# Preparing the next layer's first block inside the last image of the layer before it

## The chip, the cores and the metric

One core of one Trainium2 chip runs the whole program. The metric is the time of one execution on the device in microseconds (us), as the median of several runs. The engines are TensorE (PE), VectorE (DVE), ScalarE (ACT), GpSimd (POOL) and SyncE (SP), which here only issues DMA transfers. Each engine runs its own instructions strictly in order.

## The reference

The input x has shape (4, 56, 56, 128), and all is in float32. Four layers follow one another; the change lies at the seam between the first two.

```python
x = x + _L0_conv_ref(_gn(x), ...)     # layer 0: neighbourhood attention, 4 heads, 7x7 windows
x = x + _L1_conv_ref(_gn(x), ...)     # layer 1: two Mamba blocks, one after the other
t = _to_tokens(x)
t = t + _L2_attn_ref(_ln_t(t), ...)   # layer 2: additive (tanh) attention, then a mixture
t = t + _L2_ffn_ref(_ln_t(t), ...)
t = t + _L3_attn_ref(_ln_t(t))        # layer 3: attention, then a mixture of 8 experts
t = t + _L3_ffn_ref(_ln_t(t), ...)
```

`_gn` is a group norm over 32 groups of 4 channels. Each image has statistics of its own, so layer 1 can begin on image 0 as soon as layer 0 has finished image 0. One Mamba block of layer 1, cut to what matters:

```python
xz = h @ in_w;  u, res = split(xz, 2)
u = silu(causal_conv4(u) + cb)              # 4 taps along a row
dt, Bm, Cm = split(u @ xw, [8, 24])
delta = softplus(dt @ dtw + dtb)
h_t = exp(delta * A) * h_(t-1) + (delta * u) * Bm     # the scan, 256 channels x 16 states
y = sum over states (h_t * Cm) + u * D
return (y * silu(res)) @ ow
```

## The kernel before, in words

An image is held as 28 tiles of 112 rows and is worked on in chunks of 4 tiles (448 tokens, 8 image rows), so there are 7 chunks per image and 28 in all. The engines' instructions are placed by hand: the program's order is each engine's order, except that a few first instructions of layer 1 which depend on nothing late slip into the end of layer 0.

**Layer 0.** Each chunk k is split into two units, by columns; 56 units in all. The loop over positions i does, in this order: the scores of unit i+1 on PE (`scores`); steps listed in `early` and `turns`; their exponentials on ACT and their product with a bias table, 3 heads on DVE and 1 on POOL (`weights`); steps listed in `mid`; the weighted sums of unit i-1 on PE (`sums`); steps listed in `at`. The lists are filled ahead of the loop with queries, keys and values of later chunks; with `finish` of earlier ones, which copies the sums on ACT, divides on DVE, projects on PE and adds to X on DVE; with the group norm of the next image (`norm_steps`); and with the building of layer 1's weights on DVE (`next_weights`, 42 steps spread over 50 positions from position 4 on). The last image occupies units 42 to 55. During it, `next_norm` takes the statistics of image 0 for layer 1: 7 turns (4 transposes on PE and one statistics instruction on DVE each) at positions 42 to 48, and the group sums and the square root after them. Queries, keys, values, turns and projections share two PSUM buffers named m, in order of issue. The normalized images `xnT` lie in two buffers of the pool `l0_big`; the three bias tables tab0 to tab2 lie in `l0_w`.

**Layer 1.** A block is one chunk of one image in one of the two Mamba layers: 56 blocks, in groups of 4 and 3 chunks. Each block has 16 pairs, a pair being two sets of 8 channels with 16 states each on 128 partitions. The loop over pairs p does: the fetch of pair p+4 by DMA (E from delta_dram, or V from du_dram for 3 pairs in 16); the spreading of du on PE and the exponential of E on ACT for pair p+2 (`select`); the product with Bm on DVE for pair p+1 (`inputs`); the scan on DVE and the product with Cm on POOL for pair p (`scan`). `mamba_pre` prepares a block while the 16 pairs of the block before it run: convolution (`conv`, `conved`), SiLU, x projection (`xproj`, `dbl`), four spreads on PE with their copies (`spread`, `parts`, `spreaded`), softplus (`delta`), the product du on POOL, eight stores of du and delta to DRAM on SP (`du`), and the gate branch (`res`, `resed`). Its steps are dealt to positions relative to the block; for block 0 there are no pairs beside which they could run, so the loop begins at pair -19 and the first scan comes at pair 0.

The buffers of a block (us, delta, du, bc, sres) are in the pool `l1_sm`, two of each, used in turn; raw, raw_res and dbl have one each.

Of the kernel before, what the change touches and what calls it, by code (L numbers as in the profile page):

```python
# [20 lines left out]
P = 128  # L21
# [13 lines left out]
BW = 8  # L35
# [103 lines left out]
class Hybrid:  # L139
# [59 lines left out]
    def group_norm(self, b, pool, group):  # L199
# [12 lines left out]
        def place_bands(pool):  # L212

            g.xn = self.t(pool, [P, BANDS, HW, BW], "xnT")
            g.chunk = lambda c: g.xn[:, :, c * SEQ : (c + 1) * SEQ, :].rearrange(
                "p b s j -> p b (s j)"
            )
# [83 lines left out]
    def bias_tables(self, pool, tmp, room, m, groups):  # L301

        nc, a = self.nc, self.a
        N = sum(WIDTHS)
        K = BW * (1 + KR)
        rpb = self.load(tmp, [NH * KR, KR], "rpb", a["L0_conv_rpb"].rearrange("h r d -> (h r) d"))
        same = self.load(tmp, [K, BW], "same", a["k_same"])
        cols = self.load(tmp, [K, N], "cols", a["k_cols"])  # L310
        kill = self.load(tmp, [TP, 3 * SEQ], "kill", a["k_kill"])
        tables = [self.t(pool, [TP, NH, SEQ, N], f"tab{k}") for k in range(3)]
        often = self.t(tmp, [NH * KR, BW, 1 + KR], "rpb_often")
        nc.vector.memset(often, 1.0)
        span = ROWS + SEQ - 1 + 2 * NB
        r = {}

        def spread():

            r["rows"] = by_row = room()[:K, : NH * span * BW].rearrange(  # L320
                "p (h r k) -> p h r k", h=NH, k=BW
            )
            nc.gpsimd.memset(by_row, 0.0)
            nc.vector.tensor_copy(
                often[:, :, 0:KR], rpb.unsqueeze(1).to_broadcast([NH * KR, BW, KR])
            )
            ps = m()
            nc.tensor.transpose(
                ps[:K, : NH * KR], often.rearrange("p k d -> p (k d)"),
                self.ident[: NH * KR, : NH * KR],  # L330
            )
            for h in range(NH):
                nc.vector.tensor_tensor(
                    by_row[:, h, SEQ - 1 : SEQ - 1 + KR, :],
                    ps[:K, h * KR : (h + 1) * KR].unsqueeze(2).to_broadcast([K, KR, BW]),
                    same.unsqueeze(1).to_broadcast([K, KR, BW]), op=ALU.mult,
                )

        def table(kind, i):

            ps = groups()[:, : NH * N].rearrange("p (h n) -> p h n", h=NH)
            at = SEQ - 1 - i + (2 - kind) * NB
            for h in range(NH):
                nc.tensor.matmul(
                    ps[:, h, :], r["rows"][:, h, at : at + ROWS, :].rearrange("p r k -> p (r k)"), cols,
                    start=True, stop=True,
                )
            nc.scalar.activation(
                tables[kind][:, :, i, :], ps, AF.Exp, bias=kill[:, kind * SEQ + i : kind * SEQ + i + 1]
            )  # L350

        return tables, spread, table

    def layer0(self, wp1):
# [5 lines left out]
        with ExitStack() as ctx:  # L360
            wp = ctx.enter_context(tc.tile_pool(name="l0_w", bufs=1))
            big = ctx.enter_context(tc.tile_pool(name="l0_big", bufs=2))
# [39 lines left out]
            def norm_steps(b):  # L402
                g = self.group_norm(b, big, group)

                def chunk(c):
                    if c == 0:
                        g.place_bands(big)
                    g.turn(c, m)
                    g.stats(c)
                    return lambda: g.raw_bands(c)  # L410
# [14 lines left out]
            def next_norm():  # L425
                g = self.first_norm = self.group_norm(0, wp1, group)
                parts = g.groups(m)
                both = lambda fs: lambda: [f() for f in fs]
                def chunk(c):
                    return lambda: (g.turn(c, m), g.stats(c)) and None  # L430

                return (
                    [chunk(c) for c in range(NCH)]
                    + [parts[0], both(parts[1:3]), both(parts[3:5]), parts[5]]
                )
# [155 lines left out]
            for k, (b, c) in enumerate(chunks):  # L591
                if c == 0:
                    for n, step in enumerate(norm_steps(b + 1) if b + 1 < B else next_norm()):
                        add(first[k] + n, step, to=turns if n < NCH else at)
# [11 lines left out]
            for n, step in enumerate(next_weights):  # L606
                add(first[2] + n * 50 // len(next_weights), step)
# [124 lines left out]
    def layer1(self):  # L732
# [5 lines left out]
        with ExitStack() as ctx:  # L738
# [4 lines left out]
            dr = ctx.enter_context(tc.tile_pool(name="l1_dram", bufs=2, space=DRAM))  # L743
# [14 lines left out]
            h = {}  # L758
            pre, yg, E, D, V, HS, py = {}, {}, {}, {}, {}, {}, {}
# [147 lines left out]
            for j, block in enumerate(order):  # L907
# [24 lines left out]
                head, tail = self.mamba_pre(pre, j, block, h, w, sm, m, dr)  # L932
                for steps, to in ((head, first), (tail, last)):
                    for i, step in steps:
                        add(to, at - PAIRS + i, step)
            g = self.first_norm
            g.place(big, DC - 1)
            hand_over(0, g)
            for c in range(NCH):
                turned = lambda c=c: (g.turn(c, m), g.scaled(c, g.ps))  # L940
                if c == 0:
                    turned()
                else:
                    add(last, (-PAIRS + 9, 2, 10, 12, PAIRS + 2, PAIRS + 10)[c - 1], turned)
            for n, step in enumerate(self.first_stats()):
                add(first if n < 20 else last, n_pairs if n < 20 else n_pairs + 10, step)
            for p in range(-PAIRS - 3, n_pairs + PAIRS):
# [18 lines left out]
    def mamba_pre(self, pre, j, block, h, w, sm, m, dr):  # L966


        nc = self.nc
        b, c, l = block  # L970
        seqs = lambda ap: ap.rearrange("p (s t) -> p s t", t=HW)
        r = pre[j] = {}
        ps = {}

# [8 lines left out]
        def conved(f):  # L983
            if f == 0:
                r["raw"] = self.t(sm, [P, NHALF, CH], "raw", bufs=1)
            nc.scalar.activation(r["raw"][:, f], ps[0], AF.Identity, bias=w["cb"][:, l, f : f + 1])

        def silu(of, to):
            r[to] = self.t(sm, [P, NHALF, CH], to)
# [10 lines left out]
        def dbl():  # L1000
            r["dbl"] = self.t(sm, [P, CH], "dbl", bufs=1)
# [7 lines left out]
        def parts(i):  # L1009
            if i == 0:  # L1010
                r["delta"] = self.t(sm, [P, NHALF, CH], "delta")
# [3 lines left out]
        def spreaded(i):  # L1015
            if i == 0:
                r["bc"] = self.t(sm, [P, 2, CH], "bc")
# [5 lines left out]
        def du():  # L1023
            r["du"] = self.t(sm, [P, NHALF, CH], "du")
# [19 lines left out]
        def resed(f):  # L1044
            if f == 0:
                r["raw_res"] = self.t(sm, [P, NHALF, CH], "raw_res", bufs=1)
            nc.scalar.copy(r["raw_res"][:, f], ps[0])

        head = [
            (-1, conved, 0), (1, conved, 1), (2, resed, 0), (4, dbl), (5, parts, 0), (6, parts, 1),  # L1050
            (7, spreaded, 0), (9, spreaded, 1), (12, resed, 1),
        ]
        tail = [(k // 2 - 3, conv, k // DC, k % DC) for k in range(2 * DC)]
        tail += [
            (1, silu, "raw", "us"), (1, res, 0), (3, xproj), (4, spread, 0), (5, spread, 1),
            (6, spread, 2), (7, delta), (7, spread, 3), (8, du), (11, res, 1),
            (PAIRS + 1, silu, "raw_res", "sres"),
        ]
        bind = lambda f, *args: lambda: f(*args)
        return [[(x[0], bind(*x[1:])) for x in xs] for xs in (head, tail)]  # L1060
# [1060 lines left out]
def tile_hybrid(ctx, tc, a, out):  # L2121
    k = Hybrid(ctx, tc, a, out)
    with ExitStack() as ctx1:
        wp = ctx1.enter_context(tc.tile_pool(name="l1_w", bufs=1, reuse_waits="tile"))
        k.layer0(wp)
# [37 lines left out]
```

## Time and profile before

| quantity | value |
|---|---|
| median of 3 runs | 7037.23 us (7028.32 to 7045.93) |
| the profiled execution | 7044.67 us, span 7042.9 us |
| mean granted PE clock | 0.931 |
| PE, DVE, ACT, POOL busy in the span | 86%, 82%, 69%, 41% |
| last addition to X in layer 0 (DVE) begins | 374.23 us |
| first scan of layer 1 (DVE) begins | 409.64 us |
| last pair sums of layer 1 (PE) begin | 2988.7 us |

The granted clock is the share of its full clock at which PE was allowed to run in a stretch. Busy shares over the whole span say little here, since the layers have different limits: in layer 1 DVE is busy almost without a break, in layer 0 it is PE. Positions on the time line count from the start of the span.

### The profile page before, as it was taken

What the parts mean: (1) busy time and instruction counts of PE and PEld (TensorE: products, weight loads), DVE (VectorE), ACT (ScalarE), POOL (GpSimd) and SP (SyncE); (2) the same over time, 40 slices, a digit from 0 to 9 for tenths busy, and PEclk for the clock granted to TensorE, in tenths of its full rate; (3) what the DMA queues carried; (4) which work ended last, traced back from release to release, by engine and by line L of the source; (5) the groups of instructions that cost most, each with busy time, mean ns of one, the idle gap of its engine ahead of it and who ended that gap; (6) DMA issues with size and microseconds to landing.
All of it is one profiled execution on the core that took longest, in us unless ns stands there. A gap on an engine that the chain in (4) does not pass through costs nothing.

```text
span 7042.9 us, 101461 instructions
## 1 busy us (share of the span) xinstructions
PE 6058.3 (86%) x37386; PEld 2624.0 (37%) x37386; DVE 5762.5 (82%) x10108; ACT 4833.4 (69%) x4827; POOL 2853.0 (41%) x1920
## 2 busy tenths in 40 slices
PE   8889999998999999877777777777788899999998
PEld 7733332333232333232233323332333355555554
DVE  6869999999999999977878888888888753566665
ACT  5557767766767677679998998999899833322231
POOL 3359989998999999911010101000101100000000
PEclk9989989998999899889999999999899999999999
DMA  2057767776776777600000000000003304243433
GB/s 53 5 126 188 186 158 188 186 183 169 187 185 174 178 187 186 159 11 3 1 5 4 8 2 5 5 6 3 6 18 116 91 18 145 72 112 92 118 85 94
DMA packets 363446, 654.19 MB, mean 93 GB/s; under 512 B 95412, under 2 KB 211908, under 8 KB 362437
## 3 DMA queue, kind: packets, MB, share of 16 engines
q1 hardware_dynamic: 362949, 647.71, 36.5%
q8 instruction: 295, 4.83, 0.3%
q14 instruction: 202, 1.65, 0.1%
HBM read 536.78 MB, written 104.37 MB: 91 GB/s over the span
## 4 chain that ended last, share of the span: by engine, by line
PE 22%; ACT 12%; DVE 11%; issue 8%; POOL 1%; SPq 0%; DMA 0%; DVEq 0%; ACTq 0%; POOLq 0%
ACT th L1265 10%; PE o L1903 6%; DVE th L1256 6%; PE q L1891 5%; PE s L1279 4%; DVE X L2103 2%; PE pe L2098 2%; ACT e L1293 1%; POOL e L1300 1%; PE o L1309 1%; PE m L1437 1%; DVE wide L1923 1%; PE m L1212 1%; DVE X L1445 0%; PE m L1720 0%
## 5 line engine op out<-in xcount | busy, mean ns | idle before, releaser
L1265 ACT ACTIVATE th<-th 128x5488 f32<-128x5488 f32 (+13 forms) x560 | 2184.6, 3945 | 177.3 <-DVE th L1256 151.0
L1256 DVE TENSOR_SCALAR th<-fT,g 128x784 f32<-128x784 f32 (+13 forms) x3920 | 1868.8, 549 | 306.1 <-PE s L1279 287.7
L846 POOL TENSOR_TENSOR hs<-hs,bc 128x896 f32<-128x896 f32 x896 | 1855.2, 2090 | 125.4 <-DVE hs L841 121.6
L1279 PE MATMUL s<-th,place 128*32 128x392 f32 (+5 forms) x14112 | 1389.4, 488 | 444.5 <-ACT th L1265 441.7
L841 DVE TENSOR_TENSOR_SCAN hs<-E,u 128x896 f32<-128x896 f32 x728 | 1449.6, 2007 | 1.8 <-ACT E L825 1.8
L825 ACT ACTIVATE E<-E,rate 128x448 f32<-128x448 f32 x1456 | 886.0, 661 | 124.1 <-DMA E<-delta_dram 117.0
L1279 PEld LDWEIGHTS s<-th,place 128*32 128x32 f32 (+1 forms) x14112 | 454.1, 111 | 1313.7 <-ACT th L1265 670.4
L787 PE MATMUL u<-du,pick 32*128 32x448 f32 x2912 | 815.9, 628 | 142.7 <-DVE hs L841 139.5
L834 DVE TENSOR_TENSOR u<-u,bc 128x896 f32<-128x896 f32 x728 | 784.0, 1077 | 71.5 <-PE u L787 71.2
L1896 ACT ACTIVATE e<-q,shift 128x448 f32<-128x448 f32 (+1 forms) x511 | 322.5, 634 | 673.5 <-PE q L1891 651.3
L1300 POOL TENSOR_TENSOR e<-e,later 112x112 f32<-112x112 f32 x112 | 154.1, 1376 | 1133.4 <-ACT e L1293 676.3
L2103 DVE SCALAR_TENSOR_TENSOR X<-pe,r_gate,X 112x128 f32<-112x128 f32 x896 | 311.9, 348 | 313.9 <-PE pe L2098 277.9
L852 PE MATMUL y<-hs,sum 128*32 128x448 f32 x3584 | 499.5, 631 | 4.0 <-POOL hs L846 4.0
L1891 PE MATMUL q<-xT 128*128 128x448 f32 (+1 forms) x1022 | 500.8, 572 | 0.9 <-ACT e L1896 0.9
L1903 PE MATMUL o<-e,xk 128*128 128x448 f32 (+1 forms) x1022 | 479.5, 553 | 16.7 <-ACT oT L1868 16.7
L1309 PE MATMUL o<-e,xk 112*128 112x392 f32 (+5 forms) x1024 | 390.0, 501 | 91.2 <-POOL e L1300 87.6
L787 PEld LDWEIGHTS u<-du,pick 32*128 32x128 f32 x2912 | 246.1, 195 | 575.5 <-DVE hs L841 222.3
L1196 POOL MEMSET xa<- 112x4 f32 (+1 forms) x32 | 55.1, 1723 | 972.8 <-PE m L1189 972.8
L2032 POOL MEMSET lc_xa<- 112x4 f32 x28 | 3.1, 110 | 949.1 <-DVE lc_xa L2026 700.2
L834 POOL TENSOR_TENSOR V<-V,bc 128x896 f32<-128x896 f32 x168 | 350.3, 2085 | 12.7 <-DMA V<-du_dram 12.7
L829 ACT ACTIVATE u<-u 128x896 f32<-128x896 f32 x168 | 151.9, 904 | 294.9 <-PE u L778 215.4
L841 DVE TENSOR_TENSOR_SCAN hs<-u,V 128x896 f32<-128x896 f32 x168 | 338.3, 2014 | 0.0
(274 smaller groups left out, 7841.7 us busy)
## 6 DMA issues: line engine op xcount, KB each, us to landing
E<-delta_dram SPq DMA_DIRECT2D x728, 448.0 KB
V<-du_dram SPq DMA_DIRECT2D x168, 448.0 KB
wide<-in_L_ffn_weight SPq DMA_DIRECT2D x64, 1024.0 KB
r<-M SPq DMA_DIRECT2D x189, 224.0 KB
M<-wide SPq DMA_DIRECT2D x72, 392.0 KB
du_dram<-du SPq DMA_DIRECT2D x224, 112.0 KB
delta_dram<-delta SPq DMA_DIRECT2D x224, 112.0 KB
M<-wide SPq DMA_DIRECT2D x72, 168.0 KB
```

Source lines behind the costliest of these rows:

```text
L787: nc.tensor.matmul(halves(to)[:, k], w["pick"][own, q, :], pre[j]["du"][own, f], start=True, stop=True,)
L825: nc.scalar.activation(e, e, AF.Exp, scale=rate)
L834: eng.tensor_mul(v, v, pre[p // PAIRS]["bc"][:, 0:1].to_broadcast([P, 2, CH]))
L841: nc.vector.tensor_tensor_scan(flat, E.pop(p), V.pop(p), 0.0, op0=ALU.mult, op1=ALU.add)
L846: nc.gpsimd.tensor_mul(HS[p], HS[p], bc[:, 1:2].to_broadcast([P, 2, CH]))
L852: nc.tensor.matmul(py[j, f][r * HD : (r + 1) * HD, :], w["sum"][:, q, :], HS[p + r // 2][:, r % 2], start=False, stop=(q == QG - 1),)
L1256: nc.vector.tensor_scalar(th[i][:, s, lo:hi], fT[j][:, lo:hi], g[b, J // WT][:, at : at + 1], None, op0=ALU.add,)
L1265: nc.scalar.activation(own, own, AF.Tanh)
L1279: nc.tensor.matmul(ps[j, J][QW * blk : QW * blk + rows, h, lo:hi], place[:, off : off + rows], z[:, at + s, h * HALF + lo : h * HALF + hi] ...
L1309: nc.tensor.matmul(po[j][:, h, lo:hi], xk[b, J // WT][:, J % WT, :], e[:, h * HALF + lo : h * HALF + hi], start=(J == 0), stop=(J == t + ( ...
L1891: nc.tensor.matmul(ps[:n, :CH], of_tile(xT[b], t), xT[b][:, c * CH : (c + 1) * CH], start=True, stop=True,)
L1903: nc.tensor.matmul(po[b, c], xk[b][:n, t, :], e[:n], start=first, stop=last)
```

## The change

Two tiles of 128 partitions x 3136 elements, room0 and room1, are made in the pool that holds layer 1's weights, so that they live through both layers. In layer 0, room0 holds the normalized images 0 and 2 (`l0_big` has one buffer left, for images 1 and 3), and room1 holds bias table 0. During the last image, `hold_block` takes both rooms over for layer 1. From then on room0 holds us, delta and du of every even block and dbl of all blocks; room1 holds bc and sres of every even block and raw_res of all blocks. Odd blocks have one buffer of each in `l1_sm`. The buffer raw is gone: `conved` writes us, and the SiLU works in place.

`next_norm` is extended by block 0's preparation. Its turns stand at positions 42 to 45, the group norm's steps at 46 to 49, `place` (which normalizes chunk 0 into the part of room0 that will hold du) at 50, then one step per position: conv(0), conv(1), res(0) with the SiLU, res(1), xproj, spread(0), spread(1), spread(2) with softplus, and at 59 du with spread(3). Layer 1's loop begins at pair -4. Layer 1's weights are built over 40 positions instead of 50.

```diff
-            g.xn = self.t(pool, [P, BANDS, HW, BW], "xnT")
+            g.xn = room().rearrange("p (b s j) -> p b s j", b=BANDS, j=BW)
...
-        tables = [self.t(pool, [TP, NH, SEQ, N], f"tab{k}") for k in range(3)]
+        first = self.rooms[1]()[:TP, : NH * SEQ * N].rearrange("p (h s n) -> p h s n", h=NH, s=SEQ)
+        tables = [first] + [self.t(pool, [TP, NH, SEQ, N], f"tab{k}") for k in range(1, 3)]
...
-            big = ctx.enter_context(tc.tile_pool(name="l0_big", bufs=2))
+            big = ctx.enter_context(tc.tile_pool(name="l0_big", bufs=1))
...
-                        g.place_bands(big)
+                        g.place_bands(self.rooms[0] if b % 2 == 0 else lambda: self.t(big, [P, HW * HW], "xnT"))
...
+                def place():
+                    self.hold_block()
+                    rows = self.du_room[:, : SEQ * (DC - 1 + HW)].rearrange(
+                        "p (s t) -> p s t", t=DC - 1 + HW
+                    )
+                    nc.gpsimd.memset(rows[:, :, : DC - 1], 0.0)
+                    g.chunk = lambda c: rows[:, :, DC - 1 :]
+                    g.turn(0, m)
+                    g.scaled(0, g.ps)
+                    self.h[0, 0, 0] = rows
+
+                s = self.first_block = self.mamba_pre(0, (0, 0, 0), None, m)
+                conv = lambda f: lambda: ([s.conv(f, k) for k in range(DC)], s.conved(f))
+                return [
+                    *[chunk(c) for c in range(NCH)],
+                    parts[0], both(parts[1:3]), both(parts[3:5]), parts[5], place,
+                    conv(0), conv(1), lambda: (s.res(0), s.resed(0), s.silu("us")),
+                    lambda: (s.res(1), s.resed(1)), lambda: (s.xproj(), s.dbl()),
+                    lambda: (s.spread(0), s.parts(0)), lambda: (s.spread(1), s.parts(1)),
+                    lambda: (s.spread(2), s.spreaded(0), s.delta()),
+                    lambda: (s.du(), s.spread(3), s.spreaded(1)),
+                ]
...
+            for n, step in enumerate(next_norm()):
+                i = first[NCH * (B - 1)]
+                add(i + n // 2 if n < NCH else i + n - 3, step, to=at if n % 2 and n < NCH else mid)
...
-                add(first[2] + n * 50 // len(next_weights), step)
+                add(first[2] + n * 40 // len(next_weights), step)
...
-                head, tail = self.mamba_pre(pre, j, block, h, w, sm, m, dr)
-                for steps, to in ((head, first), (tail, last)):
-                    for i, step in steps:
-                        add(to, at - PAIRS + i, step)
+                made = self.mamba_pre(j, block, sm, m) if j else self.first_block
+                add(last, at + 1, made.silu, "sres")
+                if j:
+                    for steps, to in zip(made.dealt(), (first, last)):
+                        for i, step in steps:
+                            add(to, at - PAIRS + i, step)
...
-                    add(last, (-PAIRS + 9, 2, 10, 12, PAIRS + 2, PAIRS + 10)[c - 1], turned)
+                add(last, (-4, 2, 10, 12, PAIRS + 2, PAIRS + 10)[c - 1], turned)
...
-            for p in range(-PAIRS - 3, n_pairs + PAIRS):
+            for p in range(-4, n_pairs + PAIRS):
...
+    def hold_block(self):
+        a, b = self.rooms[0](), self.rooms[1]()
+        of = lambda t, i: t[:, i * NHALF * CH : (i + 1) * NHALF * CH].rearrange("p (f q) -> p f q", f=NHALF)
+        self.held = dict(
+            us=of(a, 0), delta=of(a, 1), du=of(a, 2), bc=of(b, 0), sres=of(b, 1), raw_res=of(b, 2),
+            dbl=a[:, 3 * NHALF * CH :],
+        )
+        self.du_room = a[:, 2 * NHALF * CH : 3 * NHALF * CH]
...
+        def home(name):
+            if j % 2 and name not in ("dbl", "raw_res"):
+                return self.t(sm, [P, NHALF, CH], name, bufs=1)
+            return self.held[name]
...
-                r["raw"] = self.t(sm, [P, NHALF, CH], "raw", bufs=1)
-            nc.scalar.activation(r["raw"][:, f], ps[0], AF.Identity, bias=w["cb"][:, l, f : f + 1])
+                r["us"] = home("us")
+            nc.scalar.activation(r["us"][:, f], ps[0], AF.Identity, bias=w["cb"][:, l, f : f + 1])
...
+        k.rooms = [lambda t=t: k.t(wp, [P, HW * HW], t) for t in ("room0", "room1")]
```

## The prediction

> **What bounds the kernel now.** I read the page first, then the stretches around the seam between layer 0 and layer 1, then each engine's timeline there. Columns of the stretches: length, busy time with instruction counts of PE, PE's weight load, VectorE (DVE), ScalarE (ACT), GpSimd (POOL), granted PE clock, DMA share, GB/s.
>
> ```profile
> 0.00:375.00 375.00, 323.44 (x5793) 262.28 (x5794) 270.26 (x371) 214.00 (x352) 127.33 (x92) 0.94 0.15 27
> 375.00:409.64 34.64, 25.52 (x51) 8.96 (x49) 2.11 (x3) 13.05 (x18) 2.23 (x3) 0.77 0.23 61
> 409.64:500.00 90.36, 80.08 (x272) 26.41 (x272) 74.36 (x50) 57.71 (x86) 70.25 (x39) 0.78 0.64 158
> 500.00:2900.00 2400.00, 2214.57 (x9225) 735.23 (x9225) 2336.80 (x1604) 1678.84 (x2543) 2277.43 (x1291) 0.91 0.74 182
> ```
>
> Layer 0 (first row) is bound by PE with DVE close behind. Layer 1 (last row) is bound by DVE, busy 97% of 2400 us: a start that comes earlier moves its whole end. Between them lie 34.6 us in which DVE works 2.1 us: block 0 of layer 1 goes through one chain across engines with nothing beside it. The third row is the ramp: DVE idles 16 us there, 17.3 us of waits all on the line that feeds its products (PE u L787).
>
> The chain in the timelines (start, length, engine, line, idle before and who ended it):
>
> ```profile
> 357.36 0.69 PE L550 MATMUL m<-wproj,oT 128*112 128x128 f32 x4 [0.71 <-DVE X L553]
> 361.88 1.20 PE L550 MATMUL m<-wproj,oT 128*112 128x128 f32 x4 [3.83 <-DVE oT L545]
> ...
> 367.78 0.37 PE L522 MATMUL d<-e,ones 112*32 112x112 f32 x8
> ...
> 373.95 4.87 PE L978 MATMUL m<-xnT,in_w 128*128 128x448 f32 x8
> 379.55 3.28 PE L978 MATMUL m<-xnT,in_w 128*128 128x448 f32 x8 [0.72 <-ACT raw L986]
> ```
>
> ```profile
> 383.51 1.28 ACT L990 ACT_TABLE_LOAD   x1
> 384.81 0.95 ACT L990 ACTIVATE us<-raw 128x896 f32<-128x896 f32 x1
> ...
> 394.62 1.28 ACT L1021 ACT_TABLE_LOAD   x1
> 395.92 0.95 ACT L1021 ACTIVATE delta<-delta 128x896 f32<-128x896 f32 x1
> ...
> 408.04 1.23 ACT L825 ACTIVATE E<-E,rate 128x448 f32<-128x448 f32 x2 [5.14 <-DMA E<-delta_dram]
> ```
>
> ```profile
> 396.94 2.08 POOL L1025 TENSOR_TENSOR du<-delta,us 128x896 f32<-128x896 f32 x1 [35.16 <-ACT delta L1021]
> ```
>
> ```profile
> 406.05 1.10 DVE L834 TENSOR_TENSOR u<-u,bc 128x896 f32<-128x896 f32 x1 [31.13 <-PE u L787]
> ...
> 409.64 3.92 DVE L841 TENSOR_TENSOR_SCAN hs<-E,u 128x896 f32<-128x896 f32 x2
> ```
>
> To see: layer 0's last sums end at 368.15 (367.78 + 0.37; I call that moment T0). Convolutions, SiLU, projections, softplus and du take to 399.0, the trip through DRAM to 408.0, and the first scan starts at 409.64, which is T0 + 41.5 us.
>
> **What goes from the seam.** The convolutions, both residual projections, SiLU, the x projection and the first spread are issued at positions 50 to 56 of the unit loop (units, for short), ahead of T0; the normalized rows come from room0. From the order of the changed kernel's instructions, behind T0 remain:
> - PE: projection of chunk 26 (0.96), then spread 1 (1.0): T0 + 1.9. ACT meanwhile copies chunk 27's sums (0.53 + 0.54), then delta's second half (0.63): T0 + 2.7.
> - PE: transposes of layer 1's chunk 1 (0.9) and spread 2 (1.0): T0 + 3.9. ACT: copy to bc (0.53), table load (1.28), softplus (0.95): T0 + 6.8.
> - From softplus to the first scan nothing changes: 409.64 - 396.87 = 12.8 us (du 2.08, eight stores of du and delta, the fetch of E, its exponential).
>
> The first scan then starts at T0 + 19.6 instead of T0 + 41.5: 21.9 us less, if T0 stays.
>
> **What it adds ahead of T0.** PE: transposes 0.6, two convolutions 2 x 3.28, two residual projections 2 x 1.0, x projection 1.8, spread 1.0: 12.0 us at full clock. Unit 50 begins at 336.4 before. From there to T0 are 31.7 us: 5.4 us are PE's idle time (0.70 + 0.18 + 0.71 + 3.83), 2.3 us a lower clock behind the 3.83 us wait, 1.4 us group-norm matmuls and transposes that now stand elsewhere. This leaves 22.6 us. DVE caused the idle time: it had the square root of the group norm (351.2 to 354.5), its mean (340.0 to 342.2) and four weight steps (0.28 each), about 7 us, in these units; the change puts them earlier. So PE sets the end: 22.6 + 12.0, plus stalls of 2.5 us (values wait for the previous chunk's addition, 1.5 us in the rows of units 43, 45 and 47, now in unit 53; a PSUM buffer that a late ACT copy releases, about 1). T0 becomes 336.4 + 37.1 = 373.5, or 5.3 us later. Gain: 21.9 - 5.3 = 16.6 us.
>
> **What is moved earlier still.** Seven turns with their statistics move from units 42 to 48 into 42 to 45. A pair of units with a turn in its odd one takes 11.8 us, without 9.7, since the turn puts the values behind DVE's addition; three such pairs become two. Against that, 5.5 us of DVE's small operations and two table loads for the square root stand in units 46 to 49, where DVE is busy 8.4 of 11.1 us per pair. I count these two as even, between -2 and +2 us for unit 50. The 42 weight steps, nearly all on DVE (0.28 to 0.39 each), end at unit 43 instead of 52: beside PE, nothing. The copies of taps on SP come sooner, and SP is idle until the stores (its longest wait is 122.6 us).
>
> On the queues: du's eight stores are SP's next entries, as before, past none; the DMA queues are nearly empty (share 0.00 at 370 to 400). On POOL du stands behind a memset of 0.26 us that may wait for DVE; DVE ends at about T0 + 6.7, when softplus ends too. The last projections wait behind three spreads, about 3 us, and only image 3 of layer 1 reads their rows, some 1900 us later. On ACT the SiLU and its two table loads (3.5 us) stand in unit 53 between the exponentials of units 54 and 55, with a values copy; behind them wait unit 55's exponential, DVE's product and the last sums. That path, 3.5 + 0.5 (copy of res) + 0.5 (values) + 1.35 + 1.2 = 7.1 us from unit 54's exponentials, has some 10 us of PE work beside it; if that cover went, it would cost up to 3.
>
> **A rule on table loads.** The row: each load takes 1.28 us (1283 ns in the group of layer 0). The Trainium skill ("ScalarE: Activation LUTs", section "Table sets: the hidden batching unit") says to batch calls by set and puts each switch at about 2.7 us; the change breaks up the exponentials with a SiLU. By that figure the path is 7.1 + 2.8 = 9.9 us against 10 of cover: nothing, just; softplus would come 1.4 us later in both kernels alike. By the row there are 3 us to spare. I take the row.
>
> **A rule on the clock.** At 405 to 416 PE ran at clock 1.00, then waited 2.5 us for a copy of raw_res inside layer 1, and from 420 to 432 it ran at 0.50 although busy 11.7 of 12 us. The Trainium skill ("TensorE: Matmul & The Clock Gate", Part 1) has the clock return after about 3.4 us of sustained activity and fall in idle windows; by it a PE kept busy across the seam enters the ramp warm, and the ramp's 17 us of DVE waits could shrink by 5 to 10 more. By the rows the low clock came after a full one and from a wait within the ramp, whose instructions stay: nothing. I take nothing, and keep 0 to 10 for the range.
>
> **The ramp and the steady part.** Layer 1 starts its loop at pair -4 instead of -19; chunk 1's work stood in pairs -3 to 12 and stays. In layer 1 the counts and durations per block are the same. One wait is new: in 27 even blocks the second copy to bc, on ACT, also waits for POOL. If it is for the products of the block two back, they ended about 9 pairs (26 us) earlier: nothing. The trace of before shows no such wait; its price lies between 0 and that of waiting for POOL's queue (below). I take 0: writes to other parts of the same rooms carry no POOL wait.
>
> **Sum.** Own time of the profiled execution 7044.67 (span 7042.9 and 1.8 around it), which is 7.4 over the median. 7044.7 - 16.6 = 7028.1; on the median 7037.2 - 16.6 = 7020.6, so 7021 us, 0.24% less. This kernel's runs spread over 0.25%, so 0.3% (21 us: under 7016 or over 7058) is what a measurement can tell from no change.
>
> **The rivals.**
> - *The preparation hides wholly and the ramp warms* (0.25). For: PE idles 5.4 us in the last units now. Against: DVE's load goes as PE's comes. With T0 as before 21.9 us, with a shorter ramp up to 30: 7007 to 7015.
> - *The cover is thin* (0.13): convolutions, values, projections and queries share two PSUM buffers in order, or PE falls to half clock for part of the units. Against: clock 1.00 from 286 to 353. Half clock over the 12 us alone adds 12: gain about 5, 7032.
> - *The shared room makes ACT wait* (0.04), slower: if the 27 new waits are for POOL's newest product, ACT, two pairs ahead of it (5.8 us), holds the exponentials queued behind that copy; with some 3 us passed on to DVE each block, 27 x 3 = 81 us less the gain: 7102. From 1.4 us a block (38 / 27) it makes the change slower beyond what can be told. Against: the dependence follows regions.
> - *The change as summed* (0.58): 12 to 21 us, 7016 to 7025.
>
> Faster by over 0.3%: the first rival and the lucky edge of the last case, 0.32. Slower 0.04. Within: 0.64. The range 7004 to 7037 takes in the first two rivals and the ramp's 0 to 10; it leaves out the slow one and a lucky or unlucky run.
>
> **What would show it.** T0 near 373 to 374 and the first scan near 393, with DVE's gap before its first product near 14 us; PE without idle stretches over 1.5 us in units 50 to 55; softplus about 7 us behind the last sums; the gaps of the ramp as before; no wait of a bc copy for POOL. Wrong if the last sums come after 380, if E's exponential waits for something other than its fetch, or if layer 1 from its first to its last scan takes more than 10 us longer or shorter.

## The result, and the profile after

| | before | after |
|---|---|---|
| median, same chip, 15 runs each | 7040.4 us | 7027.59 us |
| the profiled execution (span) | 7044.67 us (7042.9) | 7027.59 us (7025.8) |
| T0, the end of layer 0's last sums | 368.15 | 373.76 |
| first scan | 409.64 | 392.10 |
| third scan | 416.27 | 400.72 |
| last scan | 2981.59 | 2966.04 |

The ratio is 0.998 with a 95% interval of 0.9972 to 0.9988, so the change takes 8 to 20 us off. The forecast was 7021 with a range of 7004 to 7037.

The stretches of the changed kernel, cut at the same events as those shown of before (last addition to X, first scan, 90 us of ramp, the steady part):

```profile
0.00:381.00 381.00, 333.76 (x5826) 265.53 (x5827) 270.90 (x371) 224.85 (x366) 127.29 (x94) 0.96 0.16 27
381.00:392.10 11.10, 8.20 (x18) 2.65 (x16) 2.23 (x3) 3.07 (x5) 1.64 (x3) 0.78 0.71 179
392.10:482.50 90.40, 79.76 (x269) 26.38 (x270) 72.54 (x48) 58.02 (x86) 68.15 (x37) 0.77 0.63 156
500.00:2900.00 2400.00, 2213.43 (x9223) 734.86 (x9221) 2338.17 (x1605) 1683.33 (x2549) 2274.94 (x1289) 0.91 0.74 181
```

The second row is the seam: 34.64 us before, 11.10 now. PE's work in the first row grew by 10.3 us (323.44 to 333.76) while the row grew by 6. The ramp and the steady part are nearly the same rows as before.

The chain at the seam, in the timelines of PE, then ACT, then POOL, then DVE (start, length, engine, line, idle before and who ended it):

```profile
373.39 0.37 PE L540 MATMUL d<-e,ones 112*32 112x112 f32 x8
...
379.03 1.20 PE L568 MATMUL m<-wproj,oT 128*112 128x128 f32 x4 [0.90 <-DVE oT L563]
...
392.64 3.34 PE L1012 MATMUL m<-xnT,in_w 128*128 128x448 f32 x4 [3.44 <-ACT us L1020]
```

```profile
379.38 0.95 ACT L1056 ACTIVATE room<-room 128x896 f32<-128x896 f32 x1
...
390.84 1.23 ACT L844 ACTIVATE E<-E,rate 128x448 f32<-128x448 f32 x2 [6.97 <-DMA E<-delta_dram]
391.98 0.61 ACT L1020 ACTIVATE us<-m,cb 128x448 f32<-128x448 f32 x1
```

```profile
380.41 2.07 POOL L1060 TENSOR_TENSOR room<-room 128x896 f32<-128x896 f32 x1 [7.96 <-ACT room L1056]
```

```profile
386.67 1.10 DVE L853 TENSOR_TENSOR u<-u,room 128x896 f32<-128x896 f32 x1 [5.64 <-PE u L806]
...
392.10 4.04 DVE L860 TENSOR_TENSOR_SCAN hs<-E,u 128x896 f32<-128x896 f32 x2 [1.76 <-ACT E L844]
399.71 1.10 DVE L853 TENSOR_TENSOR u<-u,room 128x896 f32<-128x896 f32 x1 [3.57 <-PE u L806]
```

Softplus (L1056) begins 5.6 us behind the last sums and ends 6.6 us behind them, du follows, and the first scan comes at T0 + 18.3. Right after it a wait has grown: PE waits 3.44 us for the copy of block 1's first convolution (L1020), which on ACT stands behind the exponential of E, which waits for its fetch. DVE's gap there is 3.57 us. Before, the two were 1.26 and 1.70 us:

```profile
409.84 1.77 PE L978 MATMUL m<-xnT,in_w 128*128 128x448 f32 x4 [1.26 <-ACT raw L986]
```

```profile
415.26 1.10 DVE L834 TENSOR_TENSOR u<-u,bc 128x896 f32<-128x896 f32 x1 [1.70 <-PE u L787]
```

So a gain of 17.5 us at the first scan becomes 15.55 at the third, and from there to the last scan stays at 15.55, counted as the two executions stand.

**How the runs are compared.** The start of the program drifts by a few us from one execution to the next. The table counts from one row of scores on PE shortly before the last image, the last of form 32x104 x32 before 262 us. Where nothing ahead of T0 differs, T0 comes out alike to 0.1 us (113.9 to 114.0 in the changed kernel, conv_first and the three warm ones).

One difference ahead of that row is not drift: the spacing of the weight steps. Three stretches between rows of that form lie within images (in before 63.52 to 104.06, 121.48 to 185.66 and 203.30 to 257.42 us). Their sum is 158.84 to 159.06 us in the three kernels that build the weights over 50 positions (before, homes_only, weights50), and 160.25 to 160.36 us in the nine that build them over 40 (early7 apart, whose moved work reaches into the third stretch). The closer spacing thus costs 1.3 to 1.5 us ahead of the row. (What lies between the stretches varies by 1.8 us among the executions, whatever the spacing.) The middle stretch, before and then after, 64.18 and 64.87 us from start to start:

```profile
121.48 1.09 PE L492 MATMUL s<-q,kT 32*112 32x104 f32 x32 [1.03 <-ACT kT L457]
185.66 1.08 PE L492 MATMUL s<-q,kT 32*112 32x104 f32 x28 [0.18 <-ACT e L504]
```

```profile
122.59 1.09 PE L510 MATMUL s<-q,kT 32*112 32x104 f32 x32 [1.03 <-ACT kT L475]
187.46 1.08 PE L510 MATMUL s<-q,kT 32*112 32x104 f32 x28 [0.17 <-ACT e L522]
```

Where a kernel of the first group is compared with one of the second, these 1.3 to 1.5 us have to be added to what the table shows. Between before and after they are 1.47, so that the change's T0 is 3.2 + 1.5 = 4.7 us later, and its gain, free of drift, is 19.9 - 1.5 = 18.4 us at the first scan and 16.4 us from the third on.

After layer 1 the executions differ by up to 14 us (last scan to end of span: 4055.5 to 4069.9) in code that no kernel here changes. What is worth a few us is therefore read in the traces and not from the medians. Each trace is one execution.

| kernel | median us (before beside it) | ratio, interval | row of scores | to T0 | to first scan | first to last scan |
|---|---|---|---|---|---|---|
| before | 7040.4 | | 257.42 | 110.7 | 152.2 | 2571.95 |
| after | 7027.59 (7040.4) | 0.998 [0.9972, 0.9988] | 259.79 | 114.0 | 132.3 | 2573.94 |
| homes_only | 7043.32 (7041.59) | 1.0006 [0.9998, 1.0014] | 256.29 | 110.9 | 152.3 | 2571.93 |
| conv_twice | 7034.75 (7041.59) | 0.999 [0.9984, 0.9997] | 260.37 | 120.0 | 138.1 | 2572.14 |
| no_silu | 7026.7 (7039.45) | 0.9982 [0.9974, 0.999] | 259.07 | 113.9 | 132.4 | 2573.81 |
| weights50 | 7029.36 (7039.45) | 0.9986 [0.9979, 0.9993] | 256.15 | 116.8 | 135.6 | 2568.05 |
| early3 | 7034.78 (7039.45) | 0.9992 [0.9984, 1.0] | 260.65 | 130.4 | 148.4 | 2564.67 |
| early5 | 7044.03 (7039.45) | 1.0008 [0.9999, 1.0016] | 255.08 | 133.3 | 150.7 | 2569.27 |
| early7 | 7034.74 (7041.59) | 0.999 [0.9982, 0.9998] | | | | 2564.45 |
| conv_first | 7027.47 (7041.59) | 0.998 [0.9972, 0.9988] | 257.16 | 113.9 | 134.6 | 2571.72 |
| warm_one | 7026.74 (7039.73) | 0.998 [0.9973, 0.9988] | 259.20 | 114.0 | 132.4 | 2574.19 |
| warm_two | 7023.71 (7039.73) | 0.9975 [0.9964, 0.9986] | 260.19 | 114.0 | 132.7 | 2567.18 |
| warm_fit | 7017.13 (7038.49) | 0.9972 [0.9963, 0.9982] | 258.80 | 114.0 | 132.9 | 2563.12 |

In early7 the moved work lies ahead of that row of scores already, so it is no mark there.

### The profile page after: what moved, and what is told of

The parts are those of the page before. It is cut to its first block, busy times and chain, and to the rows that moved or that the text cites. A ratio compares the mean times of both kernels' runs of the same rounds, so it can differ in the third digit from the quotient of the medians.

```text
span 7025.8 us, 101491 instructions
## 1 busy us (share of the span) xinstructions
PE 6054.1 (86%) x37386; PEld 2622.7 (37%) x37386; DVE 5763.3 (82%) x10108; ACT 4832.9 (69%) x4828; POOL 2849.9 (41%) x1921
## 4 chain that ended last, share of the span: by engine, by line
PE 23%; ACT 12%; DVE 11%; issue 8%; POOL 1%; SPq 0%; DMA 0%; DVEq 0%; ACTq 0%; POOLq 0%
ACT th L1306 10%; PE o L1944 6%; DVE th L1297 6%; PE q L1932 5%; PE s L1320 5%; DVE X L2144 2%; PE pe L2139 2%; ACT e L1334 1%; POOL e L1341 1%; PE o L1350 1%; PE m L1478 1%; PE m L1253 1%; DVE wide L1964 1%; DVE X L1486 0%; PE m L1761 0%
## 5 line engine op out<-in xcount | busy, mean ns | idle before, releaser
L860 DVE TENSOR_TENSOR_SCAN hs<-E,u 128x896 f32<-128x896 f32 x728 | 1449.7, 2007 | 3.6 <-ACT E L844 3.6
L844 ACT ACTIVATE E<-E,rate 128x448 f32<-128x448 f32 x1456 | 886.0, 661 | 121.9 <-DMA E<-delta_dram 118.4
L865 POOL TENSOR_TENSOR hs<-hs,room 128x896 f32<-128x896 f32 x448 | 924.8, 2083 | 82.9 <-DVE hs L860 82.5
L865 POOL TENSOR_TENSOR hs<-hs,bc 128x896 f32<-128x896 f32 x448 | 926.5, 2087 | 47.3 <-DVE hs L860 45.6
L806 PE MATMUL u<-room,pick 32*128 32x448 f32 x1456 | 413.4, 638 | 68.5 <-DVE hs L860 66.7
L806 PE MATMUL u<-du,pick 32*128 32x448 f32 x1456 | 402.8, 618 | 74.2 <-DVE hs L860 72.9
L853 DVE TENSOR_TENSOR u<-u,bc 128x896 f32<-128x896 f32 x364 | 391.8, 1076 | 26.1 <-PE u L806 25.8
L853 DVE TENSOR_TENSOR u<-u,room 128x896 f32<-128x896 f32 x364 | 391.8, 1076 | 22.0 <-PE u L806 21.9
```

The lines of the kernel that those rows point to most:

```text
L806: nc.tensor.matmul(halves(to)[:, k], w["pick"][own, q, :], pre[j]["du"][own, f], start=True, stop=True,)
L844: nc.scalar.activation(e, e, AF.Exp, scale=rate)
L853: eng.tensor_mul(v, v, pre[p // PAIRS]["bc"][:, 0:1].to_broadcast([P, 2, CH]))
L860: nc.vector.tensor_tensor_scan(flat, E.pop(p), V.pop(p), 0.0, op0=ALU.mult, op1=ALU.add)
L865: nc.gpsimd.tensor_mul(HS[p], HS[p], bc[:, 1:2].to_broadcast([P, 2, CH]))
```

## The experiments

**The rooms alone: homes_only.** Rooms and fixed homes as in the changed kernel; block 0 prepared inside layer 1, with the turns and the weight steps where they were before.

```diff
-                    conv(0), conv(1), lambda: (s.res(0), s.resed(0), s.silu("us")),
...
-                    lambda: (s.du(), s.spread(3), s.spreaded(1)),
...
-            for p in range(-4, n_pairs + PAIRS):
+            for p in range(-PAIRS - 3, n_pairs + PAIRS):
```

> The two rooms and the fixed homes of even blocks, but block 0 prepared inside layer 1 as before (loop from pair -19, turns and weight steps where they were). Theory 1 (the whole effect lies in the seam; the homes cost nothing): the first scan at 409 to 411 us, the stretch from first to last scan 2574 us as in both kernels, the time equal to before within 4 us. Rival 2 (the homes or the memory's new layout give back the 2 to 4 us by which the gain of the medians, 12.8, is smaller than that of the seam, 15.5): 2 to 4 us slower than before, in waits of even blocks or behind layer 1.

The timeline of DVE in it shows the old first scan again:

```profile
408.62 3.92 DVE L840 TENSOR_TENSOR_SCAN hs<-E,u 128x896 f32<-128x896 f32 x2
```

T0, first scan and the length of layer 1 are those of before within 0.2 us. The homes by themselves cost nothing, and bring nothing. All of the change's gain lies in where block 0 is prepared, with the turns and weight steps that move along.

**More work for PE ahead of T0: conv_twice.** Block 0's two convolutions are computed twice, the first result is overwritten.

```diff
-                conv = lambda f: lambda: ([s.conv(f, k) for k in range(DC)], s.conved(f))
+                conv = lambda f: lambda: ([s.conv(f, k) for _ in range(2) for k in range(DC)], s.conved(f))
```

> The changed kernel with block 0's two convolutions each computed twice into the same accumulation buffer pool (the first result is not read): 6.6 us more PE work in the units before the last sums. Theory 1 (PE sets the end of layer 0 in the changed kernel): the last sums 5.5 to 6.6 us later than 373.8, the first scan later by the same. Rival 4 (the units are set by DVE, ACT or the exchange of PSUM buffers, so that PE work there is hidden): under 3 us later.

The last sums in the timeline of PE:

```profile
380.00 0.38 PE L540 MATMUL d<-e,ones 112*32 112x112 f32 x8
```

That is 120.0 us behind the row of scores, against 114.0: 6.0 us for 6.6 us of matmuls, and the first scan is 5.7 later. PE sets the end of layer 0; what is put on it there is paid almost in full.

**The SiLU among the exponentials: no_silu.** Block 0's SiLU is left out (an identity, with no table load, takes its place in this one block).

```diff
-            nc.scalar.activation(r[to], r[of], AF.Silu)
+            nc.scalar.activation(r[to], r[of], AF.Identity if j == 0 and to == "us" else AF.Silu)
```

> The changed kernel with the SiLU of block 0 replaced by the identity function (the SiLU is left out of one block of 56), which takes away its two table loads among layer 0's exponentials, 2.6 us on ACT. Theory 1 (PE work covers that path with about 3 us to spare): last sums within 1 us of the changed kernel, counted from the scores of unit 37. Rival (the switch holds the exponential of unit 55 and with it the last sums): 1.5 to 2.6 us earlier.

T0 and first scan move by 0.1 us each. Table loads and SiLU on ACT are covered.

**The weights of layer 1 over 50 positions again: weights50.**

```diff
-                add(first[2] + n * 40 // len(next_weights), step)
+                add(first[2] + n * 50 // len(next_weights), step)
```

> The changed kernel with layer 1's weights built over 50 positions as before, so that the last ten steps (0.28 us each on DVE) fall into the units in which block 0 is prepared. Theory 1 (PE sets these units, DVE has room): last sums and first scan within 1 us of the changed kernel, counted from the scores of unit 37. Rival (the closer spacing is needed, DVE being the bound there as it was before): 2 to 4 us later.

T0 is 2.8 us later (116.8 against 114.0). The timelines of DVE, then of PE, show how: a weight step of 0.28 us (L720) stands ahead of an addition to X, and the values (L485) wait for that addition.

```profile
346.05 0.28 DVE L720 SCALAR_TENSOR_TENSOR A_pick<-pick,A 128x128 f32<-128x128 f32 x1
346.25 0.68 DVE L571 TENSOR_TENSOR X<-m,X 112x512 f32<-112x512 f32 x1
```

```profile
346.98 0.91 PE L485 MATMUL m<-wqkv,xnT 128*112 128x128 f32 x6 [1.22 <-DVE X L571]
```

The changed kernel has no such wait there. So building the weights sooner saves 2.8 us behind the row of scores. It isn't free: ahead of that row it costs the 1.3 us told above, and about 1.5 us of T0 are left. The median can't tell so little. The profiled execution was this kernel's fastest of 16 (7021.29, against a median of 7029.36), with a layer 1 that took 6 us less than in the changed kernel (the last section).

**The same preparation earlier: early7, then early5 and early3.** These runs ask whether the preparation's 12 us of PE work are cheaper farther from the end, and whether the trip through DRAM can then run beside the last units. All steps of `next_norm` move 7, 5 or 3 positions ahead.

```diff
-                i = first[NCH * (B - 1)]
+                i = first[NCH * (B - 1)] - 7      # early7; 5 and 3 in the others
```

> The changed kernel with everything from the turns on seven positions earlier, so that du and its eight stores come at position 52 and the trip through DRAM runs beside the last units. Theory 1 (what is left of the seam is the chain from softplus through DRAM to E): the last sums of layer 0 stay at 372 to 376 us, since the same PE work stands in layer 0, and the first scan comes at 382 to 387 instead of 392, 5 to 10 us less time than the changed kernel. Rival 3 (the fetch of E is held by memory that layer 0 still uses, or the preparation earlier in the image costs layer 0 more): the first scan at 390 or later, no gain over the changed kernel.

> As early3, five positions earlier: softplus at position 53 between the exponentials of units 54 and 55, so one more pair of table loads (2.6 us on ACT), du on POOL at 54 beside DVE's products. Mended theory: worse than early3, between the changed kernel and early7 (last sums 114 and about 127 us behind the scores of unit 37), time 3 to 6 us over early3. Rival (the steps' total work matters, not where they stand): equal to early3 within 1 us.

> As early7, but only three positions earlier: the turns do not meet the group norm of image 3, softplus comes at position 55 behind the last exponential of layer 0 (no switch back of the table), du at 56. Theory 1 in its mended form (the chain behind the last sums is what is left, and it can be moved beside them only as long as it costs layer 0 nothing): last sums within 3 us of the changed kernel, counted from the scores of unit 37 (114 us there), first scan 3 to 7 us nearer, end of layer 1 and time 2 to 6 us less. Rival (any earlier place costs layer 0 more than it saves, or the chain through the last projections on PE sets the start): no gain, or a loss of 2 us and more.

All three miss; only that early5 is slower than early3 came true. T0 comes at 391.9 in early7. Counted from the row of scores it is 16.4 us later than in the changed kernel in early3, and 19.3 in early5. The timeline of PE in early3 holds the two long waits:

```profile
280.08 1.62 PE L485 MATMUL m<-wqkv,room 128*112 128x128 f32 x6 [6.65 <-DVE X L571]
...
336.99 1.62 PE L485 MATMUL m<-wqkv,xnT 128*112 128x128 f32 x6 [4.58 <-DVE X L571]
```

and the timeline of DVE what stood ahead of the second addition:

```profile
329.94 1.21 DVE L527 TENSOR_TENSOR e<-e,tab 112x1008 f32<-112x1008 f32 x1 [7.39 <-ACT e L522]
331.07 0.15 DVE L267 RECIPROCAL gn_r<-gn_r 128x1 f32<-128x1 f32 x1
331.25 0.67 DVE L268 TENSOR_TENSOR gn_q<-gn_r 128x1 f32<-128x1 f32 x1
331.96 1.21 DVE L269 TENSOR_TENSOR gn_q<-gn_q,gn_ve 128x1 f32<-128x1 f32 x1
...
336.25 0.68 DVE L571 TENSOR_TENSOR X<-m,X 112x512 f32<-112x512 f32 x1
```

DVE waited 7.39 us for an exponential, then did the square root of the group norm (3.3 us in all), and only then the reciprocal and the addition that PE's values wait for. In the changed kernel the same root starts at 339.51, behind that position's addition (336.53 to 337.22), and no values wait for it. From the row of scores to T0 PE is idle for 19.2 us in early3 and 11.2 in the changed kernel: 8.1 us of the 16.4 are waits. The other 8.3 are busy time, 111.2 against 102.8 us for the same work: the granted clock is lower, 0.76 from 320 to 340 and 0.94 from 340 to 360 where the changed kernel has 1.00. So the room for this work is not a matter of PE's sum alone: DVE's small operations stood in front of an addition, and PE paid for the waits and again for the low clock behind them. That the root's place is the only cause was not tried by itself; ACT's table loads moved with it.

**Block 1's convolutions ahead of the first exponential: conv_first.** This is to take away the 3.44 us wait of PE. The transposes of chunk 1, which the convolutions need, are issued ahead of the loop as well (not among the lines shown).

```diff
-                (-1, conved, 0), (1, conved, 1), (2, resed, 0)
+                (-3 if soon else -1, conved, 0), (-2 if soon else 1, conved, 1), (2, resed, 0)
...
-            tail = [(k // 2 - 3, conv, k // DC, k % DC) for k in range(2 * DC)]
+            tail = [(k // DC - 4 if soon else k // 2 - 3, conv, k // DC, k % DC) for k in range(2 * DC)]
```

> The changed kernel with both convolutions of block 1 and their copies issued before the first exponential of E instead of around it. In the changed kernel the copy of the first convolution stands on ACT behind the exponential that waits for DMA, and PE then waits 3.4 us for it; the first scan is 17.5 us earlier than before but the third only 15.6. Theory 1: PE's 3.4 us wait goes, the third scan moves up by 2 to 4 us and with it the whole of layer 1; time 2 to 4 us less than the changed kernel. Rival (the gap of DVE ahead of the third scan is PE's low clock alone): no change over 1 us.

The wait went and another took its place: PE's next product waited 3.71 us for a scan to release its buffer (L860), and then the clock fell.

```profile
393.90 1.86 PE L806 MATMUL u<-room,pick 32*128 32x448 f32 x4 [3.71 <-DVE hs L860]
```

Counted from the row of scores, the first scan came 2.3 us later, the third 1.3 us sooner, the last one at the same time. The stretches of conv_first, 12 us each:

```profile
404.00:416.00 12.00, 12.00 (x31) 3.73 (x31) 6.30 (x5) 4.63 (x8) 8.80 (x5) 0.50 0.64 164
416.00:428.00 12.00, 11.92 (x40) 3.28 (x36) 11.85 (x9) 8.15 (x12) 7.96 (x6) 0.50 0.22 55
```

PE is busy for 23.92 of 24 us, and the clock stays at 0.50 through all of it.

**Filling PE's waits: warm_one, warm_two, warm_fit.** If a wait of a few us takes the clock down, matmuls that nobody reads, put into the wait, should keep it up. They multiply block 0's us by a weight into the buffer y, which a later matmul starts afresh.

```diff
+            def warm(n):
+                if (0, 0) not in py:
+                    py[0, 0] = self.t(ps_y, [P, 512], "y")[:, :CH]
+                for _ in range(n):
+                    nc.tensor.matmul(py[0, 0], w["Dd"][:, 0, 0, :], pre[0]["us"][:, 0], start=True, stop=True)
...
+            add(last, -1, warm, 7)      # warm_one and warm_two; 4 in warm_fit
+            add(last, 2, warm, 5)       # warm_two; 4 in warm_fit
```

> Adds seven matmuls (128x128 by 448 each, about 0.45 us at full clock, 3.1 us together) that no later instruction reads, on TensorE ahead of the first matmul of block 1's second convolution, where TensorE waits 3.44 us in the changed kernel; nothing is left out. Theory 1 (a wait of a few us is what takes the granted clock down, some 10 us later): the clock of 404 to 416 us, 0.50 in the changed kernel, stays above 0.85, the gaps of VectorE that follow the third scan (1.28, 2.49, 1.55 us) shrink below 1 us each, and from first to last scan layer 1 takes 2 to 5 us less than 2573.9 us, unless the second wait (2.51 us at 401.6) takes the clock down by itself. Theory 2 (the low clock comes from load or on its own schedule, not from the wait): the clock falls to 0.50 as before or earlier, and layer 1 takes the same or up to 3 us more. The median changes by less than 0.1% either way.

> The same seven matmuls and five more (2.2 us) ahead of the transposes of layer 1's third chunk, where TensorE waits 2.51 us; nothing is left out. Theory 1 (waits take the clock down): no wait of TensorE over 1 us from 374 to 420 us, granted clock above 0.9 from 392 to 428, the gaps of VectorE from 404 to 420 below 1 us each, and from first to last scan 4 to 8 us less than 2573.9 us. Theory 2 (load or its own schedule): a stretch at 0.50 of 10 us or more between 390 and 440 all the same, layer 1 the same or up to 5 us longer.

> As warm_two, with four and four of the unread matmuls instead of seven and five, so that they fit into the waits at the clock of 0.50 that TensorE has there (3.2 us into 3.44, and 1.8 to 3.2 into 2.51); nothing is left out. If filling the waits is what matters and not the amount of work: granted clock of 0.9 or more from 396 to 420 us, VectorE's gap at the third scan back from 4.95 to about 3.6 us, and from first to last scan 2564 to 2567 us (warm_two 2567.2, the changed kernel 2573.9). If it was the amount of work: the clock falls to 0.50 between 404 and 416, and layer 1 takes about 2573 us. The median: within 0.05% of warm_two's either way.

The stretches from 392 on, in the changed kernel:

```profile
392.00:404.00 12.00, 8.92 (x22) 3.11 (x22) 8.33 (x6) 7.94 (x12) 7.34 (x4) 0.81 1.04 237
404.00:416.00 12.00, 11.58 (x28) 3.97 (x32) 8.23 (x6) 5.92 (x11) 7.55 (x5) 0.50 0.55 136
```

and in warm_fit:

```profile
392.00:404.00 12.00, 11.77 (x38) 4.75 (x38) 9.66 (x6) 9.56 (x14) 8.57 (x5) 1.00 1.04 234
404.00:416.00 12.00, 10.88 (x50) 3.77 (x48) 11.08 (x8) 9.64 (x16) 10.03 (x6) 1.00 0.82 196
```

The clock is 1.00 instead of 0.50 from 404 to 416, and DVE works 11.08 us there instead of 8.23. In warm_one the second wait (2.51 us, left open) was followed by 0.50 from 406 to 412, and layer 1 was no shorter. In warm_two no such wait was left, the clock stayed at 1.00 from 392 to 424, and layer 1 was 6.8 us shorter, though its first seven matmuls took 5.53 us where 3.44 were free, and DVE's gap at the third scan grew to 4.95 us. This was not the low clock: it was 1.00 in these 5.5 us. One such matmul appears as two instructions and takes about 0.8 us at full clock, not the 0.45 that the expectations took. The seven of warm_two and a stretch among them, then the four of warm_fit:

```profile
391.18 5.53 PE L880 MATMUL y<-room,D_diag 128*128 128x448 f32 x14
```

```profile
392.00:396.00 4.00, 4.00 (x12) 2.09 (x11) 3.48 (x3) 2.63 (x5) 0.44 (x1) 1.00 1.06 243
```

```profile
388.13 3.27 PE L880 MATMUL y<-room,D_diag 128*128 128x448 f32 x8
```

With four and four (warm_fit) DVE's gap at the third scan is 1.92 us, its waits for PE from 393 to 495 are 10.0 us (19.4 in the changed kernel), and layer 1 is 10.8 us shorter. That is more than was expected (7 to 10). One thing is shown: in this stretch the waits, not the load, take the clock down, for with more work in them it stays up. How much of the 10.8 us is the filling's own is not shown. weights50 fills nothing, its two waits are 5.31 and 2.51 us, and its layer 1 was 5.9 us shorter all the same.

warm_fit is the best version of all: 21.4 us below the runs of before beside it, where the change alone is 12.8 below its own. Resampling both sets of runs, the difference of these two is 0.3 to 14.2 us, so the medians only just tell it; the 10.8 us inside layer 1 are in the trace.

## Why the prediction was right, point by point

- *Layer 1 is bound by DVE, so an earlier start moves its end.* Held: from the third scan to the last the two kernels differ by nothing.
- *T0 5.3 us later.* Measured 4.7: 3.2 counted from the row of scores, and 1.5 ahead of it by the closer weight steps (5.6 as the executions stand, of which 0.9 is drift). Two errors offset each other here. The stretch from unit 50 on was put too long: predicted 37.1, measured 34.4 (339.37 to 373.76). Of its 2.5 us of stalls 0.85 came (the values of unit 53 waiting for X). The convolutions did run at clock 1.00, with no idle stretch over 1.5 us. And the start of unit 50 was put too early, the next point.
- *What is moved earlier, even, -2 to +2.* Unit 50 starts 2.0 us later, at the edge: 0.6 counted from the row of scores, and the 1.5 ahead of it. The weight steps, taken as nothing "beside PE", are not nothing: closer together they cost 1.3 to 1.5 us in the earlier images, and kept out of the last units they save 2.8 us (weights50). They are beside PE only as long as no addition to X stands behind them.
- *First scan at T0 + 19.6.* Measured 18.3. Softplus ended at T0 + 6.6, as summed (6.8). The stretch behind it, in which nothing was to change, took 11.8 us in place of 12.8.
- *Gain 16.6 us.* Measured, free of drift, 18.4 at the first scan and 16.4 from the third on. The longer wait of PE for L1020 gives 2 us back; the prediction took "nothing changes" behind softplus, and did not ask what else ACT has in its queue behind the exponential that waits for the fetch. That 16.4 lies so close to 16.6 is luck: the seam's chain became 23.2 us shorter instead of 21.9, T0 cost 4.7 instead of 5.3, and 2.0 were lost that the sum did not have. The path, its order and the bound of each stage were right.
- *Table loads by the row.* SiLU and loads were covered (no_silu). As the path was covered by either figure, the run doesn't tell 1.28 us from 2.7; the loads in the chain (L1056 and L844) took 1.28 us each, and softplus began right behind its own (load from 378.09, softplus at 379.38), so the row held there.
- *The clock rule counted as nothing.* Right for this change: from the third scan on DVE's gaps are the same in both kernels (1.28, 2.49, 1.55, 2.23, ...), and the wait of 2.51 us within the ramp remains. But the half of the rule by which idle windows take the clock down (the Trainium skill, "TensorE: Matmul & The Clock Gate", Part 1) holds in this ramp, and a wait of 2.51 us, shorter than the page's window of about 3.4, was followed by it (warm_one). With the waits filled layer 1 got 10.8 us shorter, just over the 5 to 10 that the prediction allowed; part of it may be phase (the last section). The change alone doesn't keep PE busy. The other half, a return after about 3.4 us of sustained activity, doesn't hold throughout. Behind the wait of 3.44 us the changed kernel's clock was 0.51 from 392.64 to 396 and 0.99 from 396 to 400; but in conv_first 24 us of work brought nothing back.
- *Fixed homes cost nothing.* Held (homes_only), and no copy to bc waits for POOL: of 112 copies at L1053, three had idle time before them, 2.5 us in all, for PE.
- *7021 against 7027.59.* Of the 6.6 us, 3.2 come from the level: the prediction stood on 7037.23, the median of three runs, and more runs of the same kernel give 7040.4. The other 3.4 are the gain as the medians have it (12.8 against 16.6, and 0.4 of rounding); the traces, free of drift, have 16.4 at the end of layer 1, and the scatter behind it (4055.5 to 4069.9) is larger than the rest.
- *The rivals.* Thin cover: no, clock 1.00 through units 50 to 55. Shared room making ACT wait: no. Hidden wholly, with a warm ramp: neither half came with this change.

## What to carry to other kernels

At a seam between two stages, count what each engine must still do after the last result of the first stage, and move the rest ahead of it even where it must be paid on the bounding engine: 23 us of chain were bought with T0 about 5 us later. Then look at each wait that remains right behind the seam, for it can cost twice: its own length, and the clock afterwards. A few matmuls put into it may help, sized from a measured one (0.8 us each here). Where work is moved into a stage that is close to balance, look at what stands in front of the operation that the bounding engine waits for, however short it is: weight steps of 0.3 us each cost 2.8 us in the last image (and spacing them closer cost 1.3 elsewhere), and a square root of 3.3 us stood before a wait of 4.58. And when kernels are compared from a mark on the time line, ask what the edit did ahead of the mark.

## What the runs showed of the hardware that was not expected

- The low clock can outlast the wait by far. After a single wait of 3.71 us PE ran at 0.50 from 404 to 428 while busy 23.92 of 24 us (conv_first). In warm_fit, waits of 0.83 and 1.12 us left the clock at 1.00, and a wait of 1.89 us was followed by 0.50. No threshold follows from this: between 376 and 380 in the changed kernel waits of 0.19 and 0.90 us were followed by 0.50 from 380 to 384.
- The ramp's length seems to be partly a matter of phase, of where the waits and the low clock fall. Of the kernels edited only ahead of T0, weights50, early3 and early7 took 2559.0 to 2559.4 us from third to last scan, 6 us less than the changed kernel (2565.3), with low-clock stretches in other places of the ramp; conv_twice took 2561.1, early5 2564.0 and no_silu 2565.3. Such a gain is not one of the edit's own place. What decides it was not tried.
- An operation's duration may depend on its neighbours. In early7 a product on DVE that mostly takes 1.21 us took 3.67 while POOL computed du beside it, and ended 1.07 us after du did, as if it had waited for it. This is one case, and no run takes du away. The timeline of DVE, then of POOL:

```profile
376.05 3.67 DVE L527 TENSOR_TENSOR e<-e,tab 112x1008 f32<-112x1008 f32 x1 [3.74 <-ACT room L1053]
```

```profile
376.57 2.08 POOL L1060 TENSOR_TENSOR room<-room 128x896 f32<-128x896 f32 x1
```
